# Output projections of both layers as seven quarter products, with sums of attention results in the freed input buffer

## The chip, the core and the metric

The kernel runs on one NeuronCore of one Trainium2 chip. Times are device microseconds (us) of one execution. A run of the profiler gives, for one execution, every instruction's start and end on each engine: PE (TensorE matmul), PEld (its weight loads), DVE (VectorE), ACT (ScalarE), POOL (GpSimd) and SP (the queue that issues most DMAs).

## What is computed

Input `x` is 4 images of 32 x 32 tokens with 768 channels. Two attention layers follow each other, each with a residual: `x = x + layer(group_norm(x))`, 12 heads of 64 channels, everything in float32. Cut to what matters here:

```
q, k, v = heads(x @ W + b)                # layer 1: then a 3x3 depthwise conv and a layer norm on each
attn    = softmax(q k^T / 8 + rel_h + rel_w)
out     = attn @ v                        # layer 1: + q
x       = x + out @ Wp + bp               # the output projection: (1024 x 768) times (768 x 768) per image
```

The last line, the output projection, is what the change rewrites. It is done 8 times (4 images, 2 layers).

## The kernel before

**Stages.** A stage is one image in one layer; there are 8, in the order (image 0, layer 0), (1, 0), (0, 1), (1, 1), (2, 0), (3, 0), (2, 1), (3, 1) (`stages`, L164). A stage has 6 items, one for each pair of heads (`items`, L165). `attend` (L663) does an item: for each half of the queries (`c`) and each group of four key tiles (`g`) it writes four score tiles (two PSUM banks each, L724 and L726), ACT takes their exponentials (L731), DVE adds them up (`acc`, L738 and L740), PE multiplies them with the values (`av`, L746). It stops four times for each group of four: twice after the scores, twice after `av`. Each stop is a **step**; an item has 16 steps, a stage 96. `rest` holds what closes a half of the queries (sums L687, result L703 to L710, finish L716); it is taken up one part at a time in the next groups, so a stage's last results are final only at about step 4 of the next stage.

**Other work between the steps.** `at(step, piece)` (L787) puts a piece of other work at a step: the next item's projections, convolutions and norms (`Pair.plan`, L596), the next stage's group norm, and the output projection of the stage before (`project`, L758). Pieces of one step run in the order in which they were put there; `project`'s are put last. PE, DVE, ACT and POOL execute in the order in which the program writes the instructions (`manual_schedule`, L140)[...]; only the order of SP's DMAs is left to the framework.

**Seven products for q, k, v.** In layer 0 the q, k, v projections already use Strassen's scheme (`sevens`, L355): two output tiles of 128 channels by two halves of 512 tokens make a 2 x 2 of quarters; each needs an inner sum over 768 channels, split in two halves of 384. Seven products of quarters replace eight. Sums of weights are made once in `mix_weights` (L256, on DVE in stage 0) and kept in DRAM (`mixed`); sums of inputs are made in `mix_tokens` (L272).

**The output projection before.** `project` does, for each of 6 output tiles `m` and 2 halves of the tokens, 6 products `halves(ps, w[:, n], os[n][:, cols])` added up in one bank; `halves` (L128) writes a product as two matmuls of 64 output rows each, and a float32 matmul shows as two instructions, so one output piece is 24 matmul instructions. DVE then adds bias and residual in one instruction (L780) and SP stores the tile. `os[n]` are the tiles `q`, which hold the attention results by then. The 12 pieces go to steps 7 to 14 of the next stage; those of the last stage run at the end. In the first layer-1 projection PE also makes a bias vector `pbias` (L770).

**PSUM.** Eight banks: a fixed pair for scores (`ps_a`), two more pairs `place_b` and `place_c` that are a scores pair during the scores and two single banks in between, one bank for `av`, one `small`. `bank(name)` (L117) hands out single banks in the order b, b, c, c behind the scores and c, c, b, b behind `av`. A scores pair needs both banks of its place to be read out.

**SBUF.** `xnp` holds two stage inputs `xn`; a stage's own is idle once its last q, k, v are made, until the stage after next is loaded (L794).

Of the kernel before, what the change touches and what calls it, by code (L numbers as in the profile page):

```python
# [9 lines left out]
F32 = mybir.dt.float32  # L10
# [3 lines left out]
ALU = mybir.AluOpType  # L14
# [31 lines left out]
def two_layers(ctx: ExitStack, tc: tile.TileContext, keep, x_in, wqkv, wproj, rels, windows, vrow, small, const, onehot, picks, out):  # L46
# [22 lines left out]
    dram = pool("dram", 1, space=bass.MemoryType.DRAM)  # L69
    xnp = pool("xnp", 2)  # L70
    wp = pool("wp", 2)
# [36 lines left out]


    place_b, place_c = Place("left"), Place("right")  # L110
    places = [place_b, place_c]

    def other_work(first, second):
        places[:] = [first, second]
        first.n = second.n = 0

    def bank(name):  # L117

        place = places[0]
        ps = place.single(name)  # L120
        if place.n % 2 == 0:
            places.reverse()
        return ps

# [50 lines left out]
    N_SUMS = 5  # L175
    mixed = [dram.tile([P, N_SUMS, NC // 2, P], F32, tag=f"mixed{u}", name=f"mixed{u}") for u in range(NC + NC // 2)]
    mixed_there = set()
# [41 lines left out]
    def load_xn(stage):  # L219
        b, layer = stage  # L220
        xn = xnp.tile([P, NC, T], F32, tag="xn", name="xn")
        src = rows(mid[b] if layer else x_in[b])
        for n in range(NC):
            nc.sync.dma_start(xn[:, n, :], src[:, n, :])
        xns[stage] = xn
# [6 lines left out]
    def load_weights(n):  # L232

        if n >= len(uses):
            return
        i, s, *some = uses[n]
        _, layer, hp = items[i]
        w = wp.tile([P, NC, P], F32, tag="wqkv", name="wqkv_t")
        weights[uses[n]] = w
        if not some:  # L240
            nc.sync.dma_start(w, wqkv[layer, hp, :, s])
        elif some[0] == 0:
            (pa, sa), (pb, sb) = two(i, s)
            nc.sync.dma_start(w[:, :3, :], wqkv[0, pb, :, sb, 3:])
            nc.sync.dma_start(w[:, 3:, :], wqkv[0, pa, :, sa, :3])
        else:
            u = hp if s == 0 else NC + hp // 2
            assert u in mixed_there
            sums = slice(2 * some[0] - 2, min(2 * some[0], N_SUMS))
            n_sums = sums.stop - sums.start  # L250
            nc.sync.dma_start(w[:, : 3 * n_sums, :].rearrange("p (a n) c -> p a n c", n=3), mixed[u][:, sums])

# [3 lines left out]
    def mix_weights(u):  # L256

        (pa, sa), (pb, sb) = two(u, 0) if u < NC else two(2 * (u - NC), 2)
        a = wp.tile([P, NC, P], F32, tag="wproj", name="mix_a")
        nc.sync.dma_start(a, wqkv[0, pa, :, sa])  # L260
        b = wp.tile([P, NC, P], F32, tag="wproj", name="mix_b")
        nc.sync.dma_start(b, wqkv[0, pb, :, sb])
        a1, a2, b1, b2 = a[:, :3, :], a[:, 3:, :], b[:, :3, :], b[:, 3:, :]
        sums = (b1, b2, ALU.add), (a1, a2, ALU.add), (a1, b2, ALU.add), (a2, b2, ALU.subtract), (b1, a1, ALU.subtract)
        for n, (x, y, op) in enumerate(sums):
            to = wp.tile([P, HALF], F32, tag="x", name="mix")
            to = to[:, : 3 * P].rearrange("p (n c) -> p n c", c=P)
            nc.vector.tensor_tensor(to, x, y, op)
            nc.sync.dma_start(mixed[u][:, n], to)
        mixed_there.add(u)  # L270
# [392 lines left out]
    def attend(pair, os):  # L663
# [12 lines left out]
        for c in range(T // QC):  # L676
# [41 lines left out]
            for g in range(0, NKT, 4):  # L718
                es = []
                for kt, place in zip(range(g, g + 4), (None, place_b, place_c, None)):  # L720
# [11 lines left out]
                    es.append(e)  # L732
                other_work(place_b, place_c)
                more()
# [8 lines left out]
                for t, e in enumerate(es):  # L743
                    kt = g + t
                    for j in range(2):
# [3 lines left out]
                        )  # L749
                other_work(place_c, place_b)  # L750
                more()
# [6 lines left out]
    def project(stage, os):  # L758

        b, layer = stage  # L760
        src, dst = rows(mid[b] if layer else x_in[b]), rows(out[b] if layer else mid[b])
        for m in range(NC):
            w = wp.tile([P, NC, P], F32, tag="wproj", name="wproj_t")
            nc.sync.dma_start(w, wproj[layer, :, :, m, :].rearrange("h p q -> p h q"))
            bias = col(BIAS[layer] + 18 + m)
            if layer:
                if b == 0:
                    ps = small_bank("pbias")
                    for n in range(NC):
                        nc.tensor.matmul(ps[:, 0:1], w[:, n, :], col(LN + 5), start=(n == 0), stop=(n == NC - 1))  # L770
                    nc.vector.tensor_tensor(pbias[:, m : m + 1], ps[:, 0:1], bias, ALU.add)
                bias = pbias[:, m : m + 1]
            for h in range(2):
                cols = slice(h * HALF, (h + 1) * HALF)
                x = wp.tile([P, HALF], F32, tag="x", name="x")
                nc.sync.dma_start(x, src[:, m, cols])
                ps = bank("proj")
                for n in range(NC):
                    halves(ps, w[:, n, :], os[n][:, cols], n == 0, n == NC - 1)
                nc.vector.scalar_tensor_tensor(x, ps, bias, x, ALU.add, ALU.add)  # L780
                nc.sync.dma_start(dst[:, m, cols], x)
                yield

# [8 lines left out]
    for k in range(1, len(stages)):  # L792
        first = (k - 1) * NC * n_steps
        at(first + n_steps, lambda k=k: load_xn(stages[k]))  # L794
        norm = group_norm(stages[k])
        for r in range(12):
            at(first + 2 * n_steps + 2 + 3 * r, lambda norm=norm: next(norm, None))
        if stages[k][1] == 0:
            mix = mix_tokens(stages[k])
            for r in range(5):  # L800
                at(first + 5 * n_steps + (r // 3 if stages[k - 1][1] else r - 8), lambda mix=mix: next(mix, None))
        elif stages[k - 1][1] == 0:
            at(first + 4 * n_steps + 6, lambda: [nc.gpsimd.memset(pad, 0.0) for pad in pads])
# [3 lines left out]

    for u, step in ((2, 2), (7, 4), (3, 18), (4, 34), (8, 36), (5, 50), (0, 56), (6, 60), (1, 66)):
        at(step, lambda u=u: mix_weights(u))
# [6 lines left out]
    for k, stage in enumerate(stages):  # L816
        steps = project(stage, oss[k])
        first = (k + 1) * NC * n_steps
        for r in range(2 * NC):
            at(first + 7 + 2 * r // 3, lambda steps=steps: next(steps, None))  # L820
    for _ in group_norm(stages[0]):
# [5 lines left out]
    for i, pair in enumerate(pairs):  # L827
        for _ in attend(pair, oss[i // NC]):
            for piece in events.pop(step, ()):
                piece()  # L830
            step += 1
    for part in rest:
        found = part(*found)
    def check():

# [9 lines left out]

    last = [piece for step in sorted(events) for piece in events.pop(step)]
    for piece in last[:2]:
        piece()
    bad = check()
    for piece in last[2:]:  # L850
        piece()
# [291 lines left out]
```

## Time and profile before

| what | value |
|---|---|
| time, median of 3 runs | 3983.66 us (3982.46 to 3984.02) |
| the profiled execution's own time | 3979.48 us |
| its span, first to last instruction | 3977.6 us |
| granted TensorE clock | 0.996 |
| PE busy | 3898.5 us, 98% |
| DVE busy | 2492.3 us, 63% |
| ACT busy | 1840.8 us, 46% |
| matmuls of `project` | 2304, 504.2 us busy, mean 593 ns |
| closing adds of `project` (L780) | 96, 750 ns each |

How to read it: busy time of an engine is the union of its instructions' times. Matmuls overlap: one lasts 593 ns, but the next starts about 215 ns later (24 of them start within 5.15 us), so that time on PE is counted by distance from start to start. A line of the groups gives source line, engine, operation, tiles (out<-in), shapes, count, then busy time, mean of one, and the idle time of the engine just before, with what ended it. A line of the timeline gives start, duration, engine, line, operation, tiles, shape, count, and in brackets how long the engine was idle and what released it.

### The profile page before, as it was taken

The page shows a single profiled execution, that of the slowest core. Times are in us where ns is not written, and L with a number is a line of the kernel's source. Part 1 is how long each engine was busy: PE and PEld are TensorE (multiplying, and loading weights), DVE is VectorE, ACT ScalarE, POOL GpSimd, SP SyncE. Part 2 cuts the span into 40 slices and gives each one's busy share as a digit, 9 for nine tenths or more (in the row PEclk, how much of TensorE's full clock was granted, in tenths as well). Part 3 has the DMA queues.
Part 4 walks back from the last instruction along what each step waited for, and adds up shares of the span by engine and source line. Part 5 has one row for each costly group of instructions (what it writes and reads, how often), then busy time and mean ns, then how long its engine had stood idle before and what let it go on. Part 6 is the DMA issues. An engine that isn't in the chain of part 4 may idle for free.

```text
span 3977.6 us, 79975 instructions
## 1 busy us (share of the span) xinstructions
PE 3898.5 (98%) x35026; PEld 1736.9 (44%) x35026; DVE 2492.3 (63%) x2794; ACT 1840.8 (46%) x2717; POOL 411.5 (10%) x776
## 2 busy tenths in 40 slices
PE   7999999999999999999899999999999999999999
PEld 3535434534344444444444445355443444434443
DVE  2455524557489984799633554245675898848883
ACT  2454424555355552455433544254542555425552
POOL 0111100110000100000011010001100011000010
PEclk9999999999999999999999999999999999999999
DMA  5343242221411312212133222423124121131122
GB/s 161 85 117 115 72 135 74 65 55 50 131 44 34 91 38 86 63 41 70 42 110 89 54 72 64 147 58 76 43 59 124 38 50 47 44 104 42 38 47 76
DMA packets 179044, 293.33 MB, mean 74 GB/s; under 512 B 22528, under 2 KB 77952, under 8 KB 178688
## 3 DMA queue, kind: packets, MB, share of 16 engines
q1 hardware_dynamic: 117248, 187.41, 15.1%
q0 software_dynamic: 61440, 100.71, 11.0%
q8 instruction: 279, 4.57, 0.5%
q14 instruction: 77, 0.63, 0.0%
HBM read 153.36 MB, written 34.01 MB: 47 GB/s over the span
## 4 chain that ended last, share of the span: by engine, by line
PE 90%; DVE 6%; DMA 2%; issue 1%; ACT 1%; POOL 0%; DVEq 0%; SPq 0%; ACTq 0%
PE qkv L131 19%; PE s L724 15%; PE av L746 15%; PE proj L131 13%; PE m3m L131 4%; PE m4m L131 4%; PE s L726 4%; PE m1m L131 4%; PE ln_c L131 3%; PE rel L566 3%; PE z L688 2%; PE m L131 2%; DVE shared L508 2%; DVE acc L740 2%; PE ln_t L544 1%
## 5 line engine op out<-in xcount | busy, mean ns | idle before, releaser
L731 ACT ACTIVATE e<-s 128x1024 f32<-128x1024 f32 x768 | 780.7, 1025 | 470.6 <-PE s L726 437.4
L724 PE MATMUL s<-q,k 64*128 64x512 f32 x3072 | 817.3, 608 | 11.1 <-ACT whole L572 7.6
L740 DVE TENSOR_TENSOR acc<-acc,e 128x1024 f32<-128x1024 f32 x576 | 705.6, 1225 | 184.9 <-ACT e L731 135.5
L131 PE MATMUL qkv<-xn,wqkv_t 128*64 128x512 f32 x3648 | 815.7, 596 | 2.9 <-DVE xn L314 2.9
L508 DVE SCALAR_TENSOR_TENSOR shared<-shared,sm 128x1056 f32<-128x1056 f32 x576 | 758.4, 1317 | 14.9
L726 PE MATMUL s<-bias,ones 64*128 64x512 f32 x1536 | 613.6, 792 | 14.5 <-DMA bias<-whole 9.6
L746 PE MATMUL av<-e,vt 128*64 128x512 f32 x2624 | 594.2, 594 | 0.0
L593 POOL DMA_DIRECT2D bias<-high x384 | 204.0, 549 | 3295.5 <-ACT high L582 3047.3
L131 PE MATMUL proj<-q,wproj_t 128*64 128x512 f32 x2304 | 504.2, 593 | 0.0
L131 PEld LDWEIGHTS qkv<-xn,wqkv_t 128*64 128x64 f32 x3648 | 253.8, 137 | 487.5 <-issue 482.2
L491 ACT ACTIVATE shared<-qkv,sm 128x512 f32<-128x512 f32 (+1 forms) x288 | 129.3, 502 | 591.2 <-PE qkv L131 591.2
L724 PEld LDWEIGHTS s<-q,k 64*128 64x128 f32 x3072 | 277.7, 187 | 281.1 <-issue 203.9
L746 PEld LDWEIGHTS av<-e,vt 128*64 128x64 f32 x2624 | 185.2, 137 | 346.7 <-issue 319.2
L738 DVE TENSOR_TENSOR acc<-e 128x1024 f32<-128x1024 f32 x96 | 117.5, 1224 | 305.0 <-ACT e L731 293.8
L131 PEld LDWEIGHTS proj<-q,wproj_t 128*64 128x64 f32 x2304 | 163.2, 137 | 316.4 <-issue 315.9
L726 PEld LDWEIGHTS s<-bias,ones 64*128 64x128 f32 x1536 | 150.0, 188 | 202.8 <-issue 194.7
L593 POOL DMA_DIRECT2D bias<-whole x384 | 206.0, 563 | 121.5 <-DVE whole L583 112.0
L681 ACT COPY weighed<-av 128x512 f32<-128x512 f32 x96 | 56.4, 587 | 301.7 <-PE av L746 301.7
L780 DVE SCALAR_TENSOR_TENSOR x<-proj,sm,x 128x512 f32<-128x512 f32 x48 | 36.1, 751 | 217.4 <-PE proj L131 213.1
L780 DVE SCALAR_TENSOR_TENSOR x<-proj,pbias,x 128x512 f32<-128x512 f32 x48 | 36.0, 750 | 216.1 <-PE proj L131 211.7
L131 PEld LDWEIGHTS ln_c<-cst,shared 128*64 128x64 f32 x2304 | 131.7, 138 | 48.9 <-issue 41.4
L131 PE MATMUL ln_c<-cst,shared 128*64 128x128 f32 x2304 | 139.7, 275 | 6.9 <-DVE shared L508 6.2
(121 smaller groups left out, 3744.8 us busy)
## 6 DMA issues: line engine op xcount, KB each, us to landing
bias<-high POOLq DMA_DIRECT2D x384, 128.0 KB, 2.8
bias<-whole POOLq DMA_DIRECT2D x384, 128.0 KB, 3.0
wqkv_t<-in_wqkv SPq DMA_DIRECT2D x78, 384.0 KB, 3.1
wqkv_t<-mixed SPq DMA_DIRECT2D x66, 384.0 KB, 3.1
wproj_t<-in_wproj SPq DMA_DIRECT2D x48, 384.0 KB, 3.8
wqkv_t<-in_wqkv SPq DMA_DIRECT2D x66, 192.0 KB, 2.5
xn<-in_x SPq DMA_DIRECT2D x24, 512.0 KB, 7.6
x<-in_x SPq DMA_DIRECT2D x48, 256.0 KB, 2.8
```

The lines of the kernel that those rows point to most:

```text
L131: nc.tensor.matmul(ps[lo : lo + D], a[:, lo : lo + D], b, start=start, stop=stop, **kw)
L491: nc.scalar.activation(self.pad[s][:, rows, there : there + src.shape[2]], src, AF.Identity, bias=col(self.column(s)))
L508: nc.vector.scalar_tensor_tensor(y, window, tap, y, ALU.mult, ALU.add)
L566: nc.tensor.matmul(ps[lo : lo + S, k * S : (k + 1) * S].rearrange("p (b c) -> p b c", b=2), rel[rows, 2 * self.layer + i, first : first + ...
L593: nc.gpsimd.dma_start(sets, some.unsqueeze(1).to_broadcast([D // 2, 2, QC]))
L688: nc.tensor.matmul(z[j * D : (j + 1) * D, :], cst[:, ONES : ONES + D], acc[:, j, :], start=True, stop=True,)
L724: nc.tensor.matmul(ps[:, j, :], k[rows, keys], q[rows, cols], start=True, stop=False)
L726: nc.tensor.matmul(ps[:, j, :], ones[rows, keys], bias[c][rows, kt // 2, :], start=False, stop=True,)
L731: nc.scalar.activation(e, ps, AF.Exp)
L738: nc.vector.tensor_tensor(acc, es[0], es[1], ALU.add)
L740: nc.vector.tensor_tensor(acc, acc, e, ALU.add)
L746: nc.tensor.matmul(av[j * D : (j + 1) * D, :], pair.vt[:, kt, j * D : (j + 1) * D], e[:, j, :], start=(kt == 0), stop=(kt == NKT - 1),)
```

## The change

- `project` becomes, for each of 3 pairs of output tiles, 7 products of quarters in place of 8. A product is 3 of the old 6 inner steps: 12 matmul instructions. `four(pair)` makes products 4, 3, 2, 5 in two banks; `three(pair)` makes 1, 7, 6 in two more. Two partial sums `u` and `w` live in SBUF; ACT copies the first product to `u`, DVE does the rest.
- Before that DVE forms, for each stage, 15 sums of attention results (`difference`, one, and `others`, four, for n = 0, 1, 2), each 128 x 512. Three kinds go to a new tile `os_sums` that takes the place of the stage's own `xn`, two are written over `os[n]`. They are put at steps 4, 5, 6 of the next stage, behind the other pieces of those steps; the products at 7, 9, 11, 13, 15, 17 (14 and 15 for the last pair if the next stage is layer 0). In the last stage the sums are at 6 to 4 steps before its end, the last one (`others(2)`) after `rest`.
- Sums of projection weights: 6 more `mix_weights`, at steps 72, 78, 84 (layer 0) and 116, 122, 130 (layer 1). The `pbias` matmuls move there.
- `bank`: the order behind `av` is now c, c, small, b, b, which uses the `small` bank as a third single.
- `xn` gets one buffer for even and one for odd stages; `load_xn` comes 4 steps later; layer 0's `mix_tokens` after a layer-0 stage moves from steps 72 to 76 to steps 68 to 70.

```diff
-    places = [place_b, place_c]
-    def other_work(first, second):
-        places[:] = [first, second]
-        first.n = second.n = 0
+    behind_scores, behind_av = (place_b, place_b, place_c, place_c), (place_c, place_c, None, place_b, place_b)
+    turn = list(behind_av)
+    def other_work(places):
+        turn[:] = places
+        place_b.n = place_c.n = 0
     def bank(name):
-        place = places[0]
...
+        place = turn.pop(0)
+        turn.append(place)
+        return place.single(name) if place else small_bank(name)
...
     def mix_weights(u):
...
+        else:
+            layer, m = divmod(2 * (u - PROJ_SUMS), NC)
+            for i, w in enumerate((a, b)):
+                nc.sync.dma_start(w, wproj[layer, :, :, m + i, :].rearrange("h p q -> p h q"))
+                if layer:
+                    ps = small_bank("pbias")
+                    for n in range(NC):
+                        nc.tensor.matmul(ps[:, 0:1], w[:, n, :], col(LN + 5), start=(n == 0), stop=(n == NC - 1))
+                    nc.vector.tensor_tensor(pbias[:, m + i : m + i + 1], ps[:, 0:1], col(BIAS[1] + 18 + m + i), ALU.add)
...
     def project(stage, os):
-        for m in range(NC):
...
-            for h in range(2):
...
-                for n in range(NC):
-                    halves(ps, w[:, n, :], os[n][:, cols], n == 0, n == NC - 1)
-                nc.vector.scalar_tensor_tensor(x, ps, bias, x, ALU.add, ALU.add)
-                nc.sync.dma_start(dst[:, m, cols], x)
...
+        def extra(i):
+            if not held:
+                held[0] = xnp.tile([P, NC, T], F32, tag=f"xn{stages.index(stage) % 2}", name="os_sums")
+            return held[0].rearrange("p n t -> p (n t)")[:, i * HALF : (i + 1) * HALF]
...
+        def difference(n):
+            nc.vector.tensor_tensor(extra(n), os[n + 3][:, first], x11(n), ALU.subtract)
+        def others(n):
+            x12, x21 = os[n][:, second], os[n + 3][:, first]
+            for to, x, y, op in (
+                (extra(n + 3), x12, x22(n), ALU.subtract), (extra(n + 6), x11(n), x22(n), ALU.add),
+                (x21, x21, x22(n), ALU.add), (x12, x12, x11(n), ALU.add),
+            ):
+                nc.vector.tensor_tensor(to, x, y, op)
+        def m(ps, pair, at, x, some=range(3), more=False):
+            w = weights[4 * pair + at // 2][:, 3 * (at % 2) : 3 * (at % 2) + 3, :]
+            for n in some:
+                halves(ps, w[:, n, :], x(n), start=not (n or more), stop=n == 2, skip_group_check=True)
...
+        def put(which, cols, x, ps, term=None):
+            bias = pbias[:, which : which + 1] if layer else col(BIAS[0] + 18 + which)
+            nc.vector.scalar_tensor_tensor(x, ps, bias, x, ALU.add, ALU.add)
+            if term is not None:
+                nc.vector.tensor_tensor(x, x, term, ALU.add)
+            nc.sync.dma_start(dst[:, which, cols], x)
+        add = lambda to, x, y, op=ALU.add: nc.vector.tensor_tensor(to, x, y, op)
+        def four(pair):
+            u, w = extra(9), extra(10)
+            b1, b2 = bank("p4p2"), bank("p3p5")
+            x21, x12 = get(2 * pair + 1, first), get(2 * pair, second)
+            m(b1, pair, 0, extra)
+            nc.scalar.copy(u, b1)
+            yield
+            m(b2, pair, 1, lambda n: extra(n + 3), range(2))
+            m(b1, pair, 2, x11, more=True)
+            m(b2, pair, 1, lambda n: extra(n + 3), range(2, 3))
+            load(4 * pair + 2)
+            add(u, u, b2)
+            add(w, u, b1, ALU.subtract)
+            put(2 * pair + 1, first, x21, b1)
+            m(b2, pair, 3, x22, more=True)
+            load(4 * pair + 3)
+            add(u, u, b2, ALU.subtract)
+            put(2 * pair, second, x12, b2)
+        def three(pair):
+            u, w = extra(9), extra(10)
+            b3, b4 = bank("p1p6"), bank("p7")
+            x11, x22 = get(2 * pair, first), get(2 * pair + 1, second)
+            m(b3, pair, 4, lambda n: extra(n + 6))
+            add(u, u, b3)
+            m(b4, pair, 5, lambda n: os[n + 3][:, first])
+            load(4 * pair + 4)
+            put(2 * pair, first, x11, b4, u)
+            m(b3, pair, 6, lambda n: os[n][:, second], more=True)
+            load(4 * pair + 5)
+            put(2 * pair + 1, second, x22, b3, w)
...
-        at(first + n_steps, lambda k=k: load_xn(stages[k]))
+        at(first + n_steps + 4, lambda k=k: load_xn(stages[k]))
...
-        for r in range(2 * NC):
-            at(first + 7 + 2 * r // 3, lambda steps=steps: next(steps, None))
+        if k + 1 == len(stages):
+            sums_at = (-8, -6, -6, -5, -5, -4)
+            products_at = range(9)
+        else:
+            sums_at = (2, 4, 4, 5, 5, 6, 6)
+            products_at = (7, 7, 9, 11, 11, 13, 15, 15, 17) if stages[k + 1][1] else (7, 7, 9, 11, 11, 13, 14, 14, 15)
...
+    last = [piece for step in sorted(events) for piece in events.pop(step)]
+    last.pop(0)()
     for part in rest:
         found = part(*found)
+    sums[-1]()
...
+    last.pop(0)()
     bad = check()
+    for piece in last:
         piece()
```

The pieces of `sums` are in this order: the first weight loads, then `difference(0)`, `others(0)`, `difference(1)`, `others(1)`, `difference(2)`, `others(2)`.

## The prediction, made before the changed kernel was run

> **What bounds the kernel now.** I read the page's busy times and chain first, then the groups, then, because averages say nothing of one stage, the timelines of PE and DVE at every place where a projection starts.
>
> ```profile
> span 3977.6 us, 79975 instructions
> PE 3898.5 (98%) x35026; PEld 1736.9 (44%) x35026; DVE 2492.3 (63%) x2794; ACT 1840.8 (46%) x2717; POOL 411.5 (10%) x776
> PE 90%; DVE 6%; DMA 2%; issue 1%; ACT 1%; POOL 0%; DVEq 0%; SPq 0%; ACTq 0%
> L131 PE MATMUL proj<-q,wproj_t 128*64 128x512 f32 x2304 | 504.2, 593 | 0.0
> L780 DVE SCALAR_TENSOR_TENSOR x<-proj,sm,x 128x512 f32<-128x512 f32 x48 | 36.1, 751 | 217.4 <-PE proj L131 213.1
> ```
>
> PE bounds it: 90% of the chain, and no idle time before any projection matmul. So an instruction less on PE counts in full, and so does every wait that PE gets. DVE is only 63% busy, but that is a mean. Where a projection starts with layer 1 as the next stage it looks like this (DVE, then PE):
>
> ```profile
> 2937.22 5.23 DVE L740 TENSOR_TENSOR acc<-acc,e 128x1024 f32<-128x1024 f32 x4 [0.51 <-ACT e L731]
> 2942.37 2.67 DVE L508 SCALAR_TENSOR_TENSOR shared<-shared,sm 128x1056 f32<-128x1056 f32 x2
> 2944.95 1.21 DVE L526 TENSOR_REDUCE lnv<-shared 128x16 f32<-128x1024 f32 x1
> 2946.28 4.02 DVE L508 SCALAR_TENSOR_TENSOR shared<-shared,sm 128x1056 f32<-128x1056 f32 x3
> 2951.05 1.23 DVE L537 TENSOR_TENSOR shared<-shared,r_ln 128x1024 f32<-128x1024 f32 x1
> 2953.58 0.75 DVE L780 SCALAR_TENSOR_TENSOR x<-proj,sm,x 128x512 f32<-128x512 f32 x1 [1.31 <-PE proj L131]
> ```
> ```profile
> 2944.78 3.60 PE L746 MATMUL av<-e,vt 128*64 128x512 f32 x16
> 2948.21 10.47 PE L131 MATMUL proj<-q,wproj_t 128*64 128x512 f32 x48
> ```
>
> To see here: these rows are steps 4 (two taps), 5 (squares, two taps), 6 (one tap), 7 (norm). DVE has no gap; when PE reaches step 7 at 2948.21, DVE is still in step 6, and is done with step 7 at 2952.28. Where layer 0 is next:
>
> ```profile
> 507.26 5.21 DVE L740 TENSOR_TENSOR acc<-acc,e 128x1024 f32<-128x1024 f32 x4 [1.70 <-ACT e L731]
> 519.53 0.75 DVE L780 SCALAR_TENSOR_TENSOR x<-proj,sm,x 128x512 f32<-128x512 f32 x1 [7.06 <-PE proj L131]
> ```
> ```profile
> 509.31 3.65 PE L746 MATMUL av<-e,vt 128*64 128x512 f32 x16
> 514.12 10.52 PE L131 MATMUL proj<-q,wproj_t 128*64 128x512 f32 x48
> ```
>
> Here DVE is idle for 7 us, but only from 512.47 on, 1.65 us before PE reaches step 7.
>
> [...] the trace has 5.15/24 = 215 ns, though each lasts 592.
>
> **The change part by part.** Sums are against the profiled execution (3979.48 us, span 3977.6 and 1.9 around it), which is 4.2 us below the median of the runs; the difference is then put on the median.
>
> *Removed.* An old piece is 24 matmuls, 5.15 us; 12 pieces are 61.8 us a stage. A product is 12 matmuls, 2.575 us; 21 are 54.1. Gain 7.7 us a stage, **61.8 us** in 8. The `pbias` matmuls only move.
>
> *A. The sums at steps 4 to 6.* 15 adds a stage. Independent ones start 0.61 us apart (L710 at 2931.28, the next at 2931.88). DVE takes them in order, behind `acc` and the step's taps. Product 4 needs `difference(2)` in its third inner step, 1.72 us after its start; before it lie ten other adds. Next layer 0: `acc` ends at 512.47, `difference(2)` at 512.4 + 10 x 0.61 + 0.69 = 519.2; PE wants it at 514.12 + 1.72 = 515.84. Stall 3.4 us; the starts of stages 4 and 5 show the same distances. Next layer 1: from 2942.37, two taps, five adds, squares and two taps, five adds, one tap, `difference(2)`: 2.6 + 3.05 + 3.9 + 3.05 + 1.3 + 0.7 = 14.7, so 2957.1; PE wants it at 2948.21 + 1.72 = 2949.93. Stall 7.2; the other three places differ by under 0.1. Together 3 x 3.4 + 4 x 7.2 = **39.0 us**. Nothing covers it: step 7 lies straight behind `av`, and `difference(2)` can't come earlier in DVE's order. Queued behind the waiting matmul is all of PE; ACT waits for PE's scores. From below 0 is excluded; from above, the whole of `others(2)` (2.4 us more a stage).
>
> *B. Product 5 behind product 3.* In `four` the last third of product 3 goes into bank b2, DVE adds b2 to `u`, and product 5 goes into b2 next. No matmul lies between. The last matmul lasts 592 ns where the next could start after 215; DVE starts 0.05 us after it (2958.73 in the rows of L780) and takes 0.69, PE follows 0.06 later (the z matmul behind `acc` at 3907.43). So 0.38 + 0.05 + 0.69 + 0.06 = 1.18 us, three times a stage. 7 stages: **24.8 us**; [...] up to 2.5 each if a tap is on DVE. In `three`, product 7 (2.6 us) hides the same add. ACT's copy of product 4 (0.59) is hidden by two thirds of product 3 (1.7).
>
> *C. The b pair.* With layer 1 next, at steps 11 and 15 three single banks are taken ahead, so b1 and b2 are both in `place_b`, which the second score tile needs. It is ready after subtract and closing add, about 2.0 us after the last matmul's start, the tile wants it after 1.4. 0.6 x 8 = **5 us**, 0 to 10. The old single closing add just fitted.
>
> *D. Weight sums.* Six more, about 6 us of DVE each (2.75 us of adds, 3.5 of waits on the stores, as the nine of before); three with `pbias` matmuls, the second of which waits for DVE to empty `small`. DVE has room there; the nine cost PE 7.7 us in stage 0. I take **4 us**, 0 to 12. `mix_tokens` (8.8 us) and the later `load_xn` I cost at nothing: DVE's idle time in layer 0 and the 14 steps up to the norm hide them. If that cover were gone, up to 5 us each.
>
> *E. The last stage.* Ten sums now lie ahead of the last four `acc` adds: result ends 3902.25, sums 3908.3, `acc` 3913.5 (before 3907.37), `difference(2)` 3914.1. Product 4 would be at that point at 3908.5, so PE stalls 5.6. Then z, then 5.3 us (as before from z to q) to the last q and 0.6 to its first sum; PE has 4.3 of work and waits about 2. Product 5 waits 1.6, the check's matmul 2.7. Two more b2 waits, small waits for weights that are reloaded within 2.6 us, and one more add before the last store: the end comes 6 us later than before where 7.7 earlier was due. Cost **13.7 us**, 5 to 20.
>
> SP's DMAs of the same steps (two loads and two stores of 256 KB per two products, as before; weight loads in smaller parts) and POOL, whose bias loads come at steps 10 to 12, are passed by no new wait that I can place: DMA is a quarter busy.
>
> Sum: -61.8 + 39.0 + 24.8 + 5 + 4 + 13.7 = **+24.7 us**. Profiled 4004; median 3983.7 + 24.7 = **4008 us**.
>
> **Rivals.**
> *Faster: the sums come in time.* If PE's arrival at step 7 is later than I read, or the sums are taken sooner, A is 10 and E 6: -61.8 + 10 + 24.8 + 5 + 4 + 6 = -12, 3972; without B's waits (a third of product 3 covering them) down to 3945. For it: DVE's mean share, and that PE loses an eighth of a known 504 us. Against it: the DVE rows above, which have no gap from step 4 on. It decides when `difference(2)` ends under 4 us late in layer-1 stages. 12%.
> *A draw*, within 8 us: gain and waits cancel with A near 25. 12%.
> *Much slower: DVE becomes the bound of the first item of layer-1 stages.* Beside 9 us of sums each projection gives DVE 15 small adds more, about 10 us, in a part that is 58% busy already (92.7 of 160 us from 2910); if taps delay the adds in B by one or two (1.3 us each) at every `four` and `three`, 4 x 6 x 1.5 = 36 us more: 4044. Against: most gaps of DVE after step 7 are waits on the projection itself, over 50 us of them. 12%.
> The forecast itself: 64%.
>
> **How the numbers follow.** 0.2% (8 us) is about what a measurement of this kernel tells from no change. Slower: 64% and 12%, 76; same 12; faster 12. The forecast's own range, from the bounds of B to E, is 3993 to 4026. To hold 8 in 10 I reach down into the draw and the near end of the faster case, and up to the much slower: 3974 to 4040.
>
> **What would show it.** Projection matmuls 2016, 441 us busy. PE idle on DVE at the first product of each stage: 3.4 us with layer 0 next, 7 with layer 1. A wait of about 0.8 us visible (1.18 with the overlap) ahead of product 5, 24 times, each ended by the add into `u`. The last z some 8 us after the last `av`. It is wrong if PE enters product 4 without a gap, or if product 5 follows without one.

## The result, and the profile after

| | before | after |
|---|---|---|
| time, median of 4 runs | 3983.06 us (3980.34 to 3984.02) | 4021.32 us (4016.83 to 4022.40) |
| ratio, with its 95% interval | 1 | 1.0096 [1.008, 1.0112] |
| profiled execution: own time / span | 3979.48 / 3977.6 us | 4021.96 / 4020.2 us |
| granted TensorE clock | 0.996 | 0.986 |

The change costs 38.3 us by the medians and 42.5 us between the two traces; forecast were 24.7. The top of the page of the changed kernel:

```profile
span 4020.2 us, 79887 instructions
PE 3865.9 (96%) x34738; PEld 1726.0 (43%) x34738; DVE 2675.0 (67%) x3088; ACT 1851.2 (46%) x2741; POOL 411.5 (10%) x776
PE 81%; DVE 14%; DMA 2%; issue 1%; ACT 1%; POOL 0%; SPq 0%; DVEq 0%
```

PE has 288 instructions less, but is idle for 154 us of its span where it was for 79; PE has nine points less of the chain and DVE eight more. The waits of PE (engine, tile and line, what it waited for; us in total, times, longest):

```profile
PE p4p L131 <- DVE os_sums L811: 38.8, 15, 5.3
PE p3p L131 <- DVE os_sums L839: 21.1, 24, 1.3
...
PE p1p L131 <- DVE os_sums L839: 2.9, 4, 0.7
...
PE s L741 <- DVE x L834: 2.0, 8, 0.3
```

Three of these are the waits that the prediction placed: product 4 on the sums (L811 is `difference`), product 5 on the add that empties b2 (L839, in the row of `p3p`), the score tile on the closing add (L834). Neither of the first two existed before. The row of `p1p` is one that it held to be covered: with layer 1 next, in the last pair, product 6 waits until DVE has emptied the bank of product 1, because DVE does adds of exponentials and a tap of the convolution first. The place of the forecast where layer 1 comes next, in the timelines of DVE and then of PE:

```profile
1005.15 2.67 DVE L525 SCALAR_TENSOR_TENSOR shared<-shared,sm 128x1056 f32<-128x1056 f32 x2
1007.73 0.68 DVE L811 TENSOR_TENSOR os_sums<-q 128x512 f32<-128x512 f32 x1
1008.34 1.28 DVE L820 TENSOR_TENSOR os_sums<-q 128x512 f32<-128x512 f32 x2
1009.54 1.28 DVE L820 TENSOR_TENSOR q<-q 128x512 f32<-128x512 f32 x2
1010.74 1.31 DVE L525 SCALAR_TENSOR_TENSOR shared<-shared,sm 128x1056 f32<-128x1056 f32 x1
1011.97 0.68 DVE L811 TENSOR_TENSOR os_sums<-q 128x512 f32<-128x512 f32 x1
```
```profile
1003.84 1.03 PE L131 MATMUL p4p<-os_sums,wproj_t 128*64 128x512 f32 x4
1008.47 1.98 PE L131 MATMUL p4p<-os_sums,wproj_t 128*64 128x512 f32 x4 [3.61 <-DVE os_sums L811]
1012.71 1.97 PE L131 MATMUL p4p<-os_sums,wproj_t 128*64 128x512 f32 x4 [2.27 <-DVE os_sums L811]
1014.47 3.45 PE L131 MATMUL p3p<-os_sums,wproj_t 128*64 128x512 f32 x8
...
1022.22 2.79 PE L131 MATMUL p3p<-q,wproj_t 128*64 128x512 f32 x12 [0.86 <-DVE os_sums L839]
```

DVE never stops; PE gets the three `difference` sums one by one. Then look at durations, not only at brackets: four matmuls take 1.03 us in the first row and 1.98 in the second, and the eight of product 3 take 3.45 (1.89 where nothing was waited for). The windows of the same place, of which the column behind the five engines is the granted clock, say why:

```profile
1004.00:1008.00 4.00, 0.86 (x5) 0.00 (x0) 3.93 (x5) 1.02 (x3) 0.00 (x0) 0.92 0.00 0
1008.00:1014.00 6.00, 3.26 (x8) 0.83 (x10) 6.00 (x10) 0.00 (x0) 0.00 (x0) 0.50 0.00 0
1014.00:1018.00 4.00, 4.00 (x12) 1.09 (x10) 2.90 (x7) 0.59 (x1) 0.00 (x0) 0.55 0.02 4
1018.00:1024.00 6.00, 5.13 (x26) 1.48 (x24) 2.04 (x3) 0.00 (x0) 0.00 (x0) 1.00 0.21 65
```

TensorE had half its clock from 1007.4 to 1017.6. The whole trace has 20 such stretches at a granted clock of 0.50 ("half clock" from here on), which make 113.5 us, against 9 and 36.1 us before. That is in no term of the prediction.

### The profile page after: what moved, and what is told of

It is laid out like the page before. It is cut to its first block, busy times and chain, and to the rows that moved or that the text cites. A ratio compares the mean times of both kernels' runs of the same rounds, so it can differ in the third digit from the quotient of the medians.

```text
span 4020.2 us, 79887 instructions
## 1 busy us (share of the span) xinstructions
PE 3865.9 (96%) x34738; PEld 1726.0 (43%) x34738; DVE 2675.0 (67%) x3088; ACT 1851.2 (46%) x2741; POOL 411.5 (10%) x776
## 4 chain that ended last, share of the span: by engine, by line
PE 81%; DVE 14%; DMA 2%; issue 1%; ACT 1%; POOL 0%; SPq 0%; DVEq 0%
PE qkv L131 17%; PE s L741 14%; PE av L763 13%; PE m3m L131 4%; PE m1m L131 4%; PE m4m L131 4%; DVE shared L525 4%; PE s L743 4%; DVE acc L757 3%; PE p3p L131 3%; PE p4p L131 3%; PE p1p L131 3%; PE ln_c L131 2%; PE rel L583 2%; PE z L705 2%; PE m L131 2%
## 5 line engine op out<-in xcount | busy, mean ns | idle before, releaser
L839 DVE TENSOR_TENSOR os_sums<-os_sums,p3p 128x512 f32<-128x512 f32 x48 | 33.0, 688 | 168.4 <-PE p3p L131 168.4
L583 PEld LDWEIGHTS rel<-q,rel 64*32 64x32 f32 x6144 | 111.7, 105 | 76.7 <-issue 56.5
L131 PE MATMUL m1m<-shared,wqkv_t 128*64 128x512 f32 x528 | 124.9, 609 | 4.3 <-DVE shared L393 4.0
L131 PE MATMUL m4m<-xn,wqkv_t 128*64 128x512 f32 x528 | 122.5, 599 | 4.0 <-issue 3.0
```

Of the source, the lines that this page charges most:

```text
L131: nc.tensor.matmul(ps[lo : lo + D], a[:, lo : lo + D], b, start=start, stop=stop, **kw)
L583: nc.tensor.matmul(ps[lo : lo + S, k * S : (k + 1) * S].rearrange("p (b c) -> p b c", b=2), rel[rows, 2 * self.layer + i, first : first + ...
```

## The experiments

**Theory** after the result: the terms for product 4 and product 5 are right, and what is missing is the half clock that follows PE's waits, in stage 1 too, where the bias matmuls went. **Rival:** the clock is a mere sign; the missing time is in more waits and in the added matmuls themselves. The kernel before was timed again beside each group of kernels, at 3980.6 to 3983.1 us; each ratio is to the kernel before beside it.

| kernel | median, us | ratio to before |
|---|---|---|
| sums earlier | 3967.69 | 0.9966 [0.9953, 0.9978] |
| product 2 between | 3995.93 | 1.0034 [1.0021, 1.0046] |
| no bias matmuls | 4006.81 | 1.0057 [1.0041, 1.0074] |
| before, bias matmuls moved | 3991.53 | 1.0027 [1.0016, 1.0037] |
| all four edits | 3935.81 | 0.9885 [0.987, 0.99] |
| waits filled | 4012.30 | 1.0074 [1.006, 1.0088] |
| last stage's sums earlier | 4014.81 | 1.0082 [1.0068, 1.0095] |
| `mix_tokens` back | 4030.05 | 1.0117 [1.0102, 1.0132] |
| bias columns apart | 3936.78 | 0.9887 [0.987, 0.9903] |
| weight sums spread | 3929.78 | 0.9869 [0.9853, 0.9885] |
| before, third bank alone | 3966.26 | 0.9963 [0.995, 0.9977] |
| a weight sum at step 75 | 3934.05 | 0.9885 [0.987, 0.99] |

### Sums earlier (step A)

```diff
-            sums_at = (2, 4, 4, 5, 5, 6, 6)
+            sums_at = (2, -9, -8, -7, -6, 4, 5)
```

The results of n = 0 and 1 are final before the stage ends, so four of the six pieces of sums can lie there. 

> Sums for n = 0 and 1 at 9 to 6 steps before the stage's end, those for n = 2 at steps 4 and 5; the rest as changed. Waits theory (the loss is PE's waits for the sums, for the add ahead of product 5, the step-1xx bias matmuls, and half clock behind long waits): the waits at product 4 of 5.3 us (layer 0 next) and 5.6 to 6.8 us (layer 1 next) vanish with the half clock behind them, -10 -28 -12 = about -50 us, 3971 us, 0.997 of before. Rival (DVE is full around layer-1 stages, so a wait removed here comes back at the next thing PE wants of DVE): only the three places with layer 0 next gain, about -12 us, 4009 us.

Measured: 53.6 us less than the changed kernel, and 0.34% less than before. Its waits on the sums, and the same place in PE's timeline:

```profile
PE p4p L131 <- DVE os_sums L811: 5.3, 1, 5.3
```
```profile
997.14 2.74 PE L131 MATMUL p4p<-os_sums,wproj_t 128*64 128x512 f32 x12
999.72 1.89 PE L131 MATMUL p3p<-os_sums,wproj_t 128*64 128x512 f32 x8
```

The one wait left is that of the last stage. Between the traces each place with layer 1 next gave 9.3 to 9.9 us, though its stall was 7.2; with layer 0 next 3.3, 5.0 and 5.0, where it was 3.3. What goes beyond the stall is the half clock, or so it seems; the next but one kernel tests that.

### Product 2 between products 3 and 5 (step B)

```diff
-            m(b2, pair, 1, lambda n: extra(n + 3), range(2))
+            m(b2, pair, 1, lambda n: extra(n + 3))
+            add(u, u, b2)
             m(b1, pair, 2, x11, more=True)
-            m(b2, pair, 1, lambda n: extra(n + 3), range(2, 3))
-            add(u, u, b2)
```

Product 3 is written whole, and product 2 lies behind it (not in the last stage's first pair, where `others(2)` comes late). 

> Product 3 whole ahead of product 2 (except for the first pair of the last stage), so that product 2 lies between product 3 and product 5. Waits theory: 23 waits of 0.86 us idle plus 0.38 of lost overlap vanish, -28 us, 3993 us. Rival (PE is held by DVE's total of small adds, or by the banks): the wait moves to product 2 behind ACT's copy or to the next scores, under -10 us, above 4011 us.

Measured: 25.4 us less. Of the 24 waits of product 5, 23 are gone; the one of the last stage's first pair (1.3 us) stays, and so do the four of product 6 (3.3 us). That is 1.10 us for each wait removed, predicted 1.18; for the 21 waits that the term of 24.8 us counted (the last stage's are in E) it makes 23.2.

### Waits filled with matmuls (half clock, or only a sign of it?)

```diff
-            m(b1, pair, 0, extra)
+            for n, fill in enumerate((0, 3, 2)):
+                if pair == 0 and stage != stages[-1] and stages[stages.index(stage) + 1][1]:
+                    for _ in range(fill):
+                        halves(b2, weights[0][:, 0, :], x11(0), skip_group_check=True)
+                m(b1, pair, 0, extra, (n,))
```

This is the changed kernel with 12 and 8 matmul instructions more, whose result nobody uses, in each of the four places with layer 1 next: 17 us of work added to PE. 

> As changed, but in the four places with layer 1 next PE runs 12 and 8 matmul instructions that nothing uses (into the bank of product 3, ahead of it) while it waits for the sums of product 4: 17 us more of PE work in all. Half-clock theory: the waits are as long, but no half clock follows them; it cost about 3 us a place, so 4009 us, and full clock in those places. Rival (the halved clock only falls where PE waits anyway, or costs nothing): 4021 us or a little more.

Measured: 9.0 us **less** than the changed kernel. The windows and the timeline of the place:

```profile
1004.00:1008.00 4.00, 2.79 (x12) 0.77 (x12) 4.00 (x7) 0.00 (x0) 0.00 (x0) 1.00 0.00 0
1008.00:1014.00 6.00, 5.71 (x28) 1.92 (x28) 4.48 (x10) 0.59 (x1) 0.00 (x0) 1.00 0.01 3
```
```profile
1004.06 1.08 PE L131 MATMUL p4p<-os_sums,wproj_t 128*64 128x512 f32 x4 [1.04 <-DVE os_sums L811]
1004.97 1.89 PE L131 MATMUL p3p<-q,wproj_t 128*64 128x512 f32 x8
1008.29 1.08 PE L131 MATMUL p4p<-os_sums,wproj_t 128*64 128x512 f32 x4 [1.44 <-DVE os_sums L811]
1009.20 1.89 PE L131 MATMUL p3p<-os_sums,wproj_t 128*64 128x512 f32 x8
```

The row at 1004.97 is filling. The last sum comes no sooner (the last part of product 4 starts 8.87 us after the first in both kernels: 999.42 to 1008.29 here, 1003.84 to 1012.71 there), but the clock stays whole (1.00), so that what follows runs in its usual 1.89 us. Each of the four places gave 2.1 to 2.5 us, 9.5 in sum. The profiled run is the fastest of this kernel's five: the traces differ by 16.2 us, and the rest lies at places without an edit (2.4 us in stage 0, 1.7 at a place with layer 0 next), where the half clock fell differently. So one place of one trace is good to about 2 us, and the medians and the four equal gains carry the reading. Since the kernel does more work and gets no sum earlier, the half clock is a cause, and its share in A, where layer 1 comes next, is 9 us.

### The last stage (step E)

```diff
-            sums_at = (-8, -6, -6, -5, -5, -4)
+            sums_at = (-8, -11, -10, -9, -8, -6)
```

> As changed, but in the last stage the sums for n = 0, 1 come 11 to 8 steps before its end and difference(2) 6 steps before, ahead of the last exponentials' adds. Waits theory: the wait of 5.3 us at the last product 4 and the half clock behind it go, -9 us, 4012 us. Rival (the last softmax chain is the later one anyway): the wait moves to the last third of product 3, -2 us, 4019 us.

Measured: 6.5 us less; between the two expectations, nearer to the first. The first stall is gone; waits of 1.8 us on `others(2)` (L820) and 1.3 on L839 remain, and the half clock with them (product 5 takes 4.25 us, where 2.79 is usual).

### The bias matmuls and weight sums of stage 1 (step D)

First without the 72 bias matmuls; `pbias` is then the bare bias, so this part of the computation is left out.

```diff
-                    for n in range(NC):
-                        nc.tensor.matmul(ps[:, 0:1], w[:, n, :], col(LN + 5), start=(n == 0), stop=(n == NC - 1))
-                    nc.vector.tensor_tensor(pbias[:, m + i : m + i + 1], ps[:, 0:1], col(BIAS[1] + 18 + m + i), ALU.add)
+                    nc.vector.tensor_copy(pbias[:, m + i : m + i + 1], col(BIAS[1] + 18 + m + i))
```

> The bias vector of layer 1's projection is the plain bias: its 72 single-column matmuls are left out (that part of the computation is missing). Half-clock theory: they cost 9.4 us of PE, 4.7 us of waits, and the half clock behind them about 8 us: -22 us, 3999 us, and no half clock between 620 and 730 us. Rival (instructions and waits alone): -13 us, 4008 us, half clock still there or without effect.

Measured: 14.5 us less, close to the rival. The half clock in that part (620 to 730 us) fell from 17.1 to 6.8 us, but PE's wait there behind the weight sums, 1.3 us in the changed kernel, grew to 5.9:

```profile
PE m1m L131 <- DVE shared L390: 5.9, 2, 3.0
```

Then the other way round, the kernel before with only the bias matmuls moved, with weight tiles `pb_a` and `pb_b` of their own (six loads more):

```diff
+    for m, step in ((0, 116), (2, 122), (4, 130)):
+        at(step, lambda m=m: make_pbias(m))
```

> The kernel before, with only its bias matmuls moved to steps 116, 122 and 130 of the run as in the change. Half-clock theory: the same instructions cost more there, by waits of some 3 us and by half clock of some 8 us: +10 us, 3994 us. Rival (the place does not matter): within 2 us of before, 3983 us.

Measured: 10.4 us more than before, for the same matmuls. In the traces stage 1 gets 18.9 us longer where they are now, and the projection that had them only 9.3 shorter. Only 3.0 us of the difference are waits, none of them on a load. The row that shows the rest:

```profile
629.41 1.50 PE L280 MATMUL pbias<-sm,pb_a 128*128 128x1 f32 x12
632.70 1.92 PE L280 MATMUL pbias<-sm,pb_b 128*128 128x1 f32 x12 [1.79 <-DVE pbias L281]
634.55 6.56 PE L757 MATMUL av<-e,shared 128*64 128x512 f32 x16
```

`av` takes 3.6 us elsewhere. Before, 12 such matmuls with one column each lay in front of 24 or 48 full ones; here 24 come with a wait between them, and PE gets the half clock (from 633.6 on; 6.56 us of `av`) although it counts as busy for 3.4 of 5.1 us.

### `mix_tokens` back (a step costed at nothing)

```diff
-                step = 5 * n_steps + r // 3 if stages[k - 1][1] else 4 * n_steps + 4 + r // 2
+                step = 5 * n_steps + (r // 3 if stages[k - 1][1] else r - 8)
```

> As changed, but the sums of inputs at the two changes from a layer-0 to a layer-0 stage are back at steps 72 to 76. If the weight sums at step 72 alone make the bias of the next item late in stage 0 (5.7 us of wait there, none in stage 4): +4 us in stage 4 and up to 4 more in stage 0, 4027 us. If the earlier input sums do: -6 in stage 0 and +4 in stage 4, 4019 us.

Measured: 8.7 us more, nearer to the first of the two expectations; of the 10.5 us between the two traces 6.0 lie in stage 0 and 2.6 in stage 4. The earlier steps are a gain of that size, next to the weight sum that now sits at 72.

### All four edits, and the rest of D

Sums earlier in all stages, product 2 between, and the two bias columns of a weight sum in one bank with one add behind them; in the last stage as in the kernel for it alone.

```diff
-                    nc.vector.tensor_tensor(pbias[:, m + i : m + i + 1], ps[:, 0:1], col(BIAS[1] + 18 + m + i), ALU.add)
...
+                nc.vector.tensor_tensor(pbias[:, m : m + 2], ps[:, 0:2], sm[:, at_ : at_ + 2], ALU.add)
```

> The early sums and product 2 between 3 and 5 together, the last stage's sums for n = 0, 1 moved to 11 to 8 steps before its end and difference(2) to 6, and the two bias vectors of a step made in two columns of one bank with one add behind both. Waits theory: the parts add up, 4021 - 53 - 25 - 9 - 3 = 3931 us, 0.987 of before, some 3 us of waits left at each start of a layer-1 stage. Rival (the waits stand in for each other: one removed, DVE's next result is late): above 3950 us.

Measured: 3935.81 us, 1.15% less than before. The gains add up: it is 85.5 us less than the changed kernel, and the three edits that were also timed alone gave 53.6 + 25.4 + 6.5 = 85.5 (the fourth, the bias columns, was not timed alone). A place with layer 0 next now is exactly 7.7 us shorter than before, the whole gain of the removed products. The part of stage 1 that has the bias matmuls still is 20 us longer, of which some 9 are their own time. Two kernels on top of it look for the rest:

```diff
+            for i, w in enumerate((a, b)):
...
+                if i == 0:
+                    nc.vector.tensor_tensor(pbias[:, m : m + 1], ps[:, 0:1], sm[:, at_ : at_ + 1], ALU.add)
+                    yield
```

> All four edits of the run before (3935.8 us), and in each of the three layer-1 weight sums the bias matmuls of the second output tile, with the five sums, one step (about 6 us) later than those of the first. Theory (the 24 bias matmuls in a row, 3 us with one column each, are what leads to the half clock in stage 1): the half-clock windows at 620 to 730 us go from 13.7 us to 5 or less and the time to about 3931. Rival (the cost is the 130 ns a bias matmul takes between dense groups and the DVE's waits on the stores, however they lie): within 2 us of 3936.

```diff
         for n, (x, y, op) in enumerate(sums):
+            if u >= PROJ_SUMS and n > 1:
+                yield
```

> As the kernel with the bias columns apart, and the last three sums of each of the six projection weight sums one step later each, so that DVE no longer waits for the stores of the sums before. Theory (stage 1 and stage 0 half 9 lose about 2 us a place because DVE stands behind the stores while PE wants its next subtract or bias add): the wait of m1m on DVE at 2.2 us and the longer wait of the bias matmul at 410 us go, 6 to 9 us less than the columns apart alone, about 3924. Rival (these waits only move): within 2 us of it.

Measured: 3936.78 and 3929.78. The first gained nothing, as its rival said; at steps 116 and 117 no other PE work lies between the columns, so they weren't apart there. The half clock from 620 to 730 us went from 13.7 to 10.2 us with it, and to 3.4 with the second, which took 7.0 us off and is the fastest of all kernels here; that is within the 6 to 9 of its theory, but the wait at 410 us that it named stayed (5.6 and 5.5 us). Timeline of PE with all four edits, with the columns apart, and with the sums spread:

```profile
654.93 1.50 PE L279 MATMUL pbias<-sm,mix_a 128*128 128x1 f32 x12
656.30 1.48 PE L279 MATMUL pbias<-sm,mix_b 128*128 128x1 f32 x12
658.03 4.47 PE L131 MATMUL m1m<-wqkv_t,shared 128*64 128x128 f32 x48 [0.25 <-DVE pbias L284]
...
667.30 4.51 PE L131 MATMUL m1m<-wqkv_t,shared 128*64 128x128 f32 x48 [2.19 <-DVE shared L398]
```
```profile
660.11 2.84 PE L131 MATMUL m1m<-wqkv_t,shared 128*64 128x128 f32 x48 [0.25 <-DVE pbias L285]
...
665.40 2.79 PE L131 MATMUL m1m<-wqkv_t,shared 128*64 128x128 f32 x48
668.98 1.50 PE L280 MATMUL pbias<-sm,mix_b 128*128 128x1 f32 x12 [0.79 <-DVE shared L450]
670.41 2.01 PE L750 MATMUL s<-q,k 64*128 64x512 f32 x4
```
```profile
659.19 2.84 PE L131 MATMUL m1m<-wqkv_t,shared 128*64 128x128 f32 x48 [0.25 <-DVE pbias L285]
...
664.48 2.79 PE L131 MATMUL m1m<-wqkv_t,shared 128*64 128x128 f32 x48
668.07 1.50 PE L280 MATMUL pbias<-sm,mix_b 128*128 128x1 f32 x12 [0.79 <-DVE shared L452]
669.49 1.13 PE L752 MATMUL s<-q,k 64*128 64x512 f32 x4
```

With all four edits both `m1m` products met half clock (4.47 and 4.51 us), one behind 24 bias matmuls in a row, one behind a wait on a DVE that stood at the stores of the weight sums (3.5 and 1.2 us in its timeline). With the columns apart, which puts the sums a step later too, both take 2.8 us already. So D has these two parts, and both are shown at this place. That kernel lost the gain again one step later, where the clock halved behind the second column (the scores at 670.41, 2.01 us); with the sums spread the same rows, behind the same wait of 0.79, kept the full clock (1.13 us). Such places make 4.7 of the 6.2 us between these two traces, so what in the spreading took 7.0 us off is not shown.

Then the weight sum of stage 0, from step 72 to 75.

```diff
-        (9, 72), (10, 78), (11, 84),
+        (9, 75), (10, 78), (11, 84),
```

> As the kernel with the weight sums spread (3929.8 us), and the first layer-0 projection weight sum at step 75 where 72 was. Theory (its two loads of 384 KB at 402 us run beside the loads of the score bias, and make the wait of the score tile on them 5.5 us where it was 2.3): that wait goes back to about 2.3 us and the time falls by 3 to 5 us, to about 3926. Rival (the bias is late for another reason): within 2 us of 3930, with the wait still at 5 us or more.

Measured: 3934.05, not faster. The wait of the scores on the bias DMA fell as expected (in the whole trace from 10.2 to 6.1 us), which fits that the sum's loads had made it longer; but DVE's stand at the stores then met a product instead, whose waits were 4.6 us in all before:

```profile
PE m3m L131 <- DVE shared L404: 11.0, 4, 7.5
```

### The third bank alone, in the kernel before

```diff
+    behind_scores, behind_av = (place_b, place_b, place_c, place_c), (place_c, place_c, None, place_b, place_b)
...
+        place = turn.pop(0)
+        turn.append(place)
+        return place.single(name) if place else small_bank(name)
```

> The kernel before with one thing of the change: the single bank small as third bank behind the values (order c, c, small, b, b). Theory (the change brought a gain that the prediction has no term for: the 18 waits of a score tile on ACT's copy of a rel bank, 7.6 us in the kernel before and none after, go with the order of banks): those waits are gone and the time is 7 to 8 us below the kernel before, about 3974. Rival (they went with the later arrival of the products or only move): within 3 us of it.

Measured: 14.5 us **less** than before, twice the theory's number. In the kernel before, the waits have the line

```profile
PE s L724 <- ACT whole L572: 7.6, 18, 0.4
```

which is gone with the new order. Each of the 18 places shows 0.42 us of idle PE, but nearly all come 0.7 us sooner: the idle time that the trace shows begins only when the last matmul has ended, as with product 5 (0.86 us of idle time, 1.10 gained). 18 x 0.7 is 12.6; the other differences between the two traces come to 2 us. The same shifts stand in the trace of the changed kernel. The change contains a gain, then, that the prediction had no term for, and so the costs that it missed are larger than 13.6 us.

## Why the prediction was right or wrong, step by step

The direction and the mechanism were right: PE waits for the sums, then for b2. The size was short by 13.6 us by the medians, and that it wasn't short by twice as much is luck: costs that the terms lacked and a gain that they lacked stood against each other. Term by term, in us:

| term | predicted | measured | from |
|---|---|---|---|
| removed products | -61.8 | -61.8 | 7.7 a place with layer 0 next, all four edits |
| A, product 4 on the sums | +39.0 | +52.0 | sums earlier, its seven places in the traces (medians: 53.6) |
| B, product 5 on b2 | +24.8 | +23.2 | product 2 between, 21 of its 23 waits |
| C, b pair for the scores | +5 | +4.0 | traces: eight places, 0.5 each |
| product 6 behind product 1 | 0 | about +4 | four waits of 0.73, and the 0.2 or so by which product 5's cost exceeds its idle time |
| D, weight sums, bias matmuls, moves | +4 | +15.5 | traces: stage 1 +22.9 less 9.1 that came with the matmuls, stage 0 +5.8, stage 4 -4.1 |
| E, last stage | +13.7 | +20.2 | traces: end 12.5 later, 7.7 earlier was due |
| third bank | 0 | -14.5 | before, third bank alone |
| sum | +24.7 | +42.6 | medians +38.3, traces +42.5 |

A, B and the third bank come from kernels of their own. D and E are what is left of their stretches when the two traces are set against each other, so that the sum comes out near the traces' difference says only that no other stretch holds a cost.

**A** had the stall right. With layer 1 next PE wanted `difference(2)` at 1003.84 + 1.72 = 1005.56 and went on at 1012.71: 7.15, predicted 7.2 (the six parts that it adds up make 14.6 as printed, not 14.7). With layer 0 next: 519.65 + 1.72 against 524.69, 3.3, predicted 3.4. The step that failed is that PE goes on at full speed afterwards. (1.97 - 1.03) for the last four matmuls of product 4 and (3.45 - 1.89) for the eight of product 3 make 2.5 us a place; four places are 10, and the filled waits gave 9.0. Two of the places with layer 0 next lost 1.7 more in the same way. The clock record of the traces of before and after holds two values only, 1.00 and 0.50. But for the one in which each trace ends, its half-clock stretches last 3.41, 6.83 or 10.24 us, and the starts within a trace lie whole multiples of 3.413 us apart. Why the clock falls is not shown.

**B** (1.10 us a wait, predicted 1.18; product 5 waited on L839 all 24 times) and the removed products were right. **C** was right within 1 us. Its waits on L834 make 2.0 us, but that is again only the idle time that shows: the second score tile starts 1.61 us after the first, where it was 1.19 before, and the third loses 0.08 more.

```profile
1110.00 1.13 PE L741 MATMUL s<-q,k 64*128 64x512 f32 x4
1111.61 1.09 PE L741 MATMUL s<-q,k 64*128 64x512 f32 x3 [0.25 <-DVE x L834]
```

What the prediction said of `three`, that product 7 hides the add into `u`, fails four times: with layer 1 next the last pair's add comes behind a tap on DVE, and product 6 waits 0.73 us for it. That wait stays in every kernel with the change.

**D** is, in proportion, the worst-sized term: "DVE has room there" was true of DVE and wrong of PE. The bias matmuls cost 10.4 us by being moved alone; with all four edits 24 of them in a row, at one column each, were followed by half clock (the product at 658.03 took 4.47 us, where it took 2.84 with the columns apart). And the weight sums make DVE stand at their stores while PE wants its next subtract. Even the bound of 12 us was too low. Beside it "costed at nothing" for `mix_tokens` was wrong in the other direction (8.7 us).

**E** also had its waits right in the main (the first stall 5.35 us, predicted 5.6; product 5's 1.33, predicted 1.6; but 0.8 for the last sum, predicted about 2) and lacked the clock. In the rows of that end

```profile
3944.12 1.97 PE L131 MATMUL p4p<-os_sums,wproj_t 128*64 128x512 f32 x4 [5.35 <-DVE os_sums L811]
3945.88 1.92 PE L705 MATMUL z<-acc,cst 128*64 128x512 f32 x4
3947.59 2.92 PE L131 MATMUL p3p<-os_sums,wproj_t 128*64 128x512 f32 x8
...
3956.27 4.49 PE L131 MATMUL p3p<-q,wproj_t 128*64 128x512 f32 x12 [1.33 <-DVE os_sums L839]
...
3963.18 4.49 PE L131 MATMUL p1p<-os_sums,wproj_t 128*64 128x512 f32 x12 [0.24 <-DVE bad L955]
```

the excess over the usual durations (1.03, 1.08, 1.89, 2.79, 2.74) is 6.3 us, and 13.7 + 6.3 = 20.0; with the shorter wait counted, about 1 us stays open.

**The third bank** was read as a cost only (C). The wait that it removes stood among PE's waits of the kernel before, at 7.6 us; the prediction went by the waits of the projection alone.

**The rivals.** The faster case needed `difference(2)` less than 4 us late; it was 7. (Its lower end of 3945 us is 3947 by its own terms.) DVE as the bound of the first item isn't seen: with the sums earlier DVE has the same work, and the time falls by 53.6 us. Of the delays by taps that this rival named, product 6's four waits are what the trace shows. The sum of the terms lies 4 us above the medians; which of them is too large by that stays open.

**What would show it** named 441 us for the projection's matmuls. The groups of products 4 and 3 show where it failed (count, busy, mean ns, idle before):

```profile
L131 PE MATMUL p3p<-os_sums,wproj_t 128*64 128x512 f32 x288 | 79.5, 664 | 0.8 <-DVE os_sums L820 0.8
L131 PE MATMUL p4p<-os_sums,wproj_t 128*64 128x512 f32 x288 | 77.7, 659 | 39.4 <-DVE os_sums L811 38.8 <-DMA wproj_t<-in_wproj 0.5
L131 PE MATMUL p4p<-q,wproj_t 128*64 128x512 f32 x288 | 65.9, 592 | 0.0
```

A group of 288 is busy for 65.9 us where no wait precedes it, and 12 to 14 us longer behind the waits. The seven groups make 492.0 us. 7 x 65.9 is 461: 441 was seven eighths of the old 504.2, whose rows held 24 or 48 matmuls, and twelve in a row of their own count for 2.74 us where a quarter of the old row of 48 is 2.63. The other 31 us come behind waits.

## What to carry to other kernels

A wait on the bounding engine can cost more than its idle time: taking out the stalls of 7.2 us with layer 1 next gave 9.3 to 9.9 a place. Around the waits of 3.61 and 2.27 us shown above, PE had half clock for 10.2 us, so look at the clock column and at the durations behind each gap, and price a wait with them. Compare starts, too, and not only idle times: a wait of 0.25 us moved the next tile by 0.42. Before a sum is made that PE wants at once, ask from which step its inputs are final; two thirds of these were, and putting them there turned 1.0096 into 0.9966. Moved matmuls aren't free because they are the same matmuls: in front of dense work these short ones cost their own 9.3 us, beside waits 18.9.

## What the runs showed of the hardware

- The clock halved in the changed kernel at 1007.4, where PE had been idle for 2.5 us, and it stayed halved behind the wait of 2.27 us. The 23 waits of 0.86 us (product 5) left it whole, the one of 1.33 in the last stage was followed by half clock (4.49 us for 12 matmuls). Whole it stayed, too, behind those of 1.04 and 1.44 with 12 and 8 matmuls between, at the place shown for the filled waits (1.00).
- The length of a wait did not decide it alone. In the changed kernel's three places with layer 0 next, product 4 has the same two waits, of 0.95 and 1.93 us: at 519.65 the clock stays whole (the eight matmuls of product 3 take 1.89 us), at 2059.50 and 2507.69 it halves (3.58 and 2.67). The kernels with columns apart and with sums spread run the same rows at two places: a wait of 0.79, then 12 matmuls of one column. In the first the clock halves behind them (four score matmuls take 2.01 and 2.08 us), in the second it doesn't (1.13 both times). What decides is not shown, and no threshold is claimed.
- Matmuls with one column kept PE busy by the profile for 1.5 us per 12 and didn't keep the clock up (all four edits: 24 of them fill 654.93 to 657.8, and the product behind them takes 4.47 us), while 20 unused full ones at each of four places made the kernel 9.0 us faster.
